# Token tiles from a block-ordered copy, constants asked for later, and six PSUM banks for the early projection

## The chip, the cores and the metric

The kernel runs on one core of one Trainium2 chip. The metric is the device time of one execution in microseconds (us), and lower is better. The engines are named as the profile names them: PE is TensorE (PEld its weight loads), DVE is VectorE, ACT is ScalarE, POOL is GpSimd and SP is SyncE, which here issues the DMA transfers.

## The reference

A transformer block on 48 x 48 tokens of 768 channels (float32 throughout) is followed by a block of Fourier mixing. Cut to what matters:

```
xn  = layernorm(x)                                  # 2304 tokens x 768
q, k, v = split(xn @ qkv_w + qkv_b)                 # 12 heads of 64
attn = softmax(q k^T / 8 + rel_h(q) + rel_w(q))     # 2304 x 2304 for each head
x   = x + (attn v) @ proj_w + proj_b
x   = x + gelu(layernorm(x) @ mlp_w1 + mlp_b1) @ mlp_w2 + mlp_b2
f   = rfft2(x)                                      # over the 48 x 48 grid
f   = softshrink(relu(f w1 + b1) w2 + b2)           # complex, 8 blocks of 96 channels
out = irfft2(f) + x
```

## The kernel before, in words

Tokens are worked on in groups of 384, six in all, and each group as three tiles of 128 rows. The order of tokens in the first stages is by blocks: group `g` holds eight rows `h` of the grid, and its tile `b` holds the sixteen columns `w` of one third of each of these rows. The view `blocks` (L180) of `x` describes this, so that one tile of 128 tokens is gathered from eight runs of sixteen tokens.

**The first stage** is `queries_keys_values`. Its order on PE and on SP is the order in which the program is written; the order on DVE, ACT and POOL is set by the framework's scheduler. `arrive(g)` asks SP for the three tiles of a group (L388, 384 KB each). `normal(t)` normalises one tile on DVE, with one small ScalarE step between: two statistics (L116), their aggregate (L118), the square root on ACT (L120), a reciprocal (L121) and the scaling (L124). `channels_first(g)` transposes the group on PE (L403, with the constant `ident`) and copies the result out of PSUM to `main` (L406 on DVE, L410 on ACT, both with the constant `vec`). `sums_of_tokens` (L172 on DVE) makes the sums of a seven-product matrix scheme from two groups, and `left` (L154 to L157 on POOL) those of the weights. `queries_and_keys` then runs the seven products (L446 on PE, four PSUM banks, emptied by L424 to L428, L455 and L457), and `values` does the same for the values (L477, L485, L487). The results go out to DRAM (L458, L489).

The queue of SP begins in this order: `ident` (L81), `vec` (L83), six token tiles (L388), and two pairs of weight loads (L364) of 384 KB each. A pair waits until a given tile has been normalised: the list `normalised` holds the L124 of each tile in order, and the two pairs wait for entries 3 and 4 (counted from 0). Later groups of tokens are asked for from within the products of the first pass, `arrive(2)` and `arrive(3)` behind a pair of weight loads, and `arrive(4)` and `arrive(5)` in the second pass.

**Attention** follows, the longest stage. It fills all PSUM banks, and the work on PE is again in written order.

**The early projection** multiplies the attention's output by `proj_w`. `outputs(t)` loads one tile of it from DRAM (L685, tile `og`, six buffers), `residual(t)` loads the tokens (L678) and adds the bias on POOL (L679), and `projected` runs two halves of six matmuls each (L692) into a PSUM tile `pp`, to which DVE adds the residual (L696). The PSUM pool of these tiles has two buffers. Nine of the eighteen tiles are done before a branch (L732), whose condition is worked out on DVE (L712 to L717), transposed on PE (L721) ahead of tile 2, and read back. The second half of the tiles and the multilayer perceptron come behind the branch, then the Fourier stages.

Of the kernel before, what the change touches and what calls it, by code (L numbers as in the profile page):

```python
# [15 lines left out]
PSUM = bass.MemoryType.PSUM  # L16
DRAM = bass.MemoryType.DRAM

P = 128
HW = 48  # L20
T = HW * HW
NT = T // P
C = 768
# [21 lines left out]
def block_then_afno(  # L45
    ctx: ExitStack,
    tc: tile.TileContext,
    x,
    qkv_w,
    proj_w,  # L50
    mlp_w1,
# [19 lines left out]
    nc = tc.nc  # L71
# [6 lines left out]

    const = ctx.enter_context(tc.tile_pool(name="const", bufs=1))
    ident = const.tile([P, P], F32, name="ident")  # L80
    nc.sync.dma_start(out=ident, in_=c_ident)  # L81
    vec = const.tile([P, V_N], F32, name="vec")
    nc.sync.dma_start(out=vec, in_=vecs)  # L83
    eps = const.tile([P, 1], F32, name="eps")
    nc.vector.memset(eps, 1e-5)
    ones = const.tile([P, P], F32, name="ones")
# [66 lines left out]
    def left(eng, a11, a12, a21, a22, s):  # L153
        eng.tensor_tensor(s[0], a21, a22, ALU.add)  # L154
        eng.tensor_tensor(s[1], s[0], a11, ALU.subtract)  # L155
        eng.tensor_tensor(s[2], a12, s[1], ALU.subtract)
        eng.tensor_tensor(a21, a11, a21, ALU.subtract)  # L157
# [19 lines left out]
        return [a[:, :, at] for a in (*blocks, *(xs[:, i] for i in range(3)))]  # L177


    blocks = x.rearrange("(a h b w) c -> a b h w c", h=8, b=3, w=16)  # L180

    def by_rows(a):

# [5 lines left out]
    with ExitStack() as flag_scope:  # L189
# [11 lines left out]
        with ExitStack() as att:  # L201
# [120 lines left out]
            def queries_keys_values(qkv):  # L322
# [38 lines left out]
                def weights_of(pr, slot, behind=None):  # L361
                    w, ws = pairs[slot]
                    for i in range(2):
                        load = nc.sync.dma_start(  # L364
                            out=w[:, :, i],
                            in_=qkv_w[:, ds(i * C + pr * P, P)].rearrange("(c p) f -> p c f", p=P),
                        )
                        if behind is not None:
                            tc.add_manual_dep(
                                load.ins, behind.ins.name,  # L370
                                mybir.DependencyInfo(
                                    mybir.DependencyClass.Sync, mybir.DependencyReason.DATA
                                ),
                                reason="tokens first",
                            )
                    left(
                        nc.gpsimd, w[:, 0:3, 0], w[:, 3:6, 0], w[:, 0:3, 1], w[:, 3:6, 1],
                        [ws[:, i] for i in range(3)],
                    )
                    return w, ws  # L380
# [3 lines left out]
                def arrive(g):  # L384

                    x3 = b_pool.tile([P, 3, C], F32, name="x3", tag="terms")
                    for i in range(3):
                        nc.sync.dma_start(out=x3[:, i], in_=blocks[g, i])  # L388
                    arrived[g] = x3

                normalised = []
# [96 lines left out]
                        t = 6 * p + 3 * (j - 1) + i  # L488
                        nc.sync.dma_start(out=v_d[ts(t, P), ts(k - 1, CH)], in_=o)  # L489

                for g in range(2):
                    arrive(g)
                for t in range(6):
                    normal(t)
                orders = []
# [6 lines left out]
                    orders.append(work)  # L502

                pairs_left = [i for work in orders for kind, i in work if kind == 0]
                ahead = [weights_of(pairs_left.pop(0), i, normalised[3 + i]) for i in range(2)]
                slot = 0
                for p in range(T // TB):
                    for g in (2 * p, 2 * p + 1):
# [29 lines left out]
            with tc.manual_schedule(engines={mybir.EngineType.PE, mybir.EngineType.SP}):  # L538
# [80 lines left out]
                with tc.manual_schedule(engines={mybir.EngineType.Activation}):  # L619
                    for n, (pr, c, u) in enumerate(runs):  # L620
# [19 lines left out]
                        if pr < NC - 1:  # L640
                            if (c, u) in ((3, 1), (4, 0), (4, 1)):
                                i = 2 * (2 * (c - 3) + u - 1)
# [33 lines left out]
        def residual(t):  # L676

            nc.sync.dma_start(out=x1[:, t, :], in_=x[ts(t, P), :])  # L678
            nc.gpsimd.tensor_tensor(x1[:, t, :], x1[:, t, :], pb, ALU.add)  # L679

        def outputs(t, og=None):

            if og is None:
                og = pj.tile([P, NC, P], F32, name="og")
            nc.sync.dma_start(out=og, in_=oT[:, ts(t, P)].rearrange("(c p) t -> p c t", p=P))  # L685
            return og

        def projected(psum, t, og):
            for k in range(2):
                pp = psum.tile([P, CH], F32, name="pp", tag="o")  # L690
                for c in range(NC):
                    nc.tensor.matmul(  # L692
                        pp, og[:, c, :], pw[:, c, ts(k, CH)], start=(c == 0), stop=(c == NC - 1)
                    )
                half = x1[:, t, ts(k, CH)]
                nc.vector.tensor_tensor(half, pp, half, ALU.add)  # L696
# [2 lines left out]

        EARLY = NT // 2  # L700
        with tc.tile_pool(name="ps_flag", bufs=1, space=PSUM) as psum, tc.tile_pool(
            name="ps_early", bufs=2, space=PSUM
        ) as psum_early, tc.manual_schedule(engines={mybir.EngineType.PE}):
            early = {t: outputs(t) for t in range(3)}
            pb = pj.tile([P, C], F32, name="pb", bufs=1)
            nc.sync.dma_start(out=pb, in_=proj_b[0, :].partition_broadcast(P))
            b2 = pj.tile([P, C], F32, name="b2_early", bufs=1)
            nc.sync.dma_start(out=b2, in_=mlp_b2[0, :].partition_broadcast(P))
            residual(0)
            projected(psum_early, 0, early[0])  # L710
            total = flag_pool.tile([P, 2], F32, name="total")
            nc.vector.tensor_reduce(total[:, 0:1], sums, AX.X, ALU.add)  # L712
            nc.vector.tensor_reduce(total[:, 1:2], inverse, AX.X, ALU.add)
            within = flag_pool.tile([P, 2], F32, name="within")
            nc.vector.tensor_scalar(within, total, BIG, None, ALU.is_lt)
            both = flag_pool.tile([P, 1], F32, name="both")
            nc.vector.tensor_tensor(both, within[:, 0:1], within[:, 1:2], ALU.mult)  # L717
            for t in range(1, EARLY):
                if t == 2:
                    line = psum.tile([1, P], F32, name="line")  # L720
                    nc.tensor.transpose(line, both, ident)  # L721
                    all_f = flag_pool.tile([1, 1], F32, name="all_f")
                    nc.vector.tensor_reduce(all_f, line, AX.X, ALU.min)
                    all_i = flag_pool.tile([1, 1], I32, name="all_i")
                    nc.vector.tensor_copy(all_i, all_f)
                residual(t)
                projected(psum_early, t, early[t] if t in early else outputs(t))
            for t in range(EARLY, NT):
                residual(t)
            later = {t: outputs(t) for t in range(EARLY, EARLY + 3)}  # L730
        safe = nc.values_load(all_i[0:1, 0:1], min_val=0, max_val=1)
        with tc.If(safe < 1):  # L732
            with ExitStack() as att:
                xnT = main.rearrange("p (c t) -> p c t", c=NC)
                with tc.tile_pool(name="g_ln1", bufs=3) as ln1, tc.tile_pool(
                    name="g_ps_ln1", bufs=2, space=PSUM
# [24 lines left out]
                for pr in range(NC):  # L761
                    w3 = []
                    for n, name in enumerate(("g_wq", "g_wk", "g_wv")):
                        w = w_pool.tile([P, NC, P], F32, name=name)
                        nc.sync.dma_start(
                            out=w,
                            in_=qkv_w[:, ds(n * C + pr * P, P)].rearrange("(c p) f -> p c f", p=P),
# [33 lines left out]
                    for sg in range(T // SG):  # L801
# [20 lines left out]
                        for i in range(2):  # L822
                            hp = psum.tile([P, G], F32, name="g_hp", tag="m")
                            for r in range(8):
                                h = sg * 16 + i * 8 + r
# [13 lines left out]
                        for i in range(2):  # L839
                            wp = psum.tile([P, 24, 16], F32, name="g_wp", tag="m")  # L840
                            for r in range(24):
                                w = i * 24 + r
# [15 lines left out]
                        for j in range(2):  # L858
                            for qt in range(SG // P):
# [27 lines left out]
                                for kg in range(NT // 3):  # L887
# [20 lines left out]
                                    out=oT[ds(pr * P + 64 * j, 64), ds(sg * SG + qt * P, P)],  # L908
                                    in_=ot[rows, :],
# [226 lines left out]
    with ExitStack() as sp:  # L1136
# [35 lines left out]
        for t in range(2):  # L1172
            nc.sync.dma_start(
                out=d2[ts(t, HW)].rearrange("p n o -> p (n o)"),
                in_=fb2[t, :].partition_broadcast(HW),
# [242 lines left out]
def _laid_out(x, given):  # L1418

    import numpy as np  # L1420

    w = {name: np.asarray(a) for name, a in given.items()}

    def columns(v):
        return v.reshape(-1, P).T

    vecs = np.concatenate(
        [
            columns(v)
            for v in (  # L1430
                w["L0_conv_ln1_g"],
                w["L0_conv_ln1_b"],
                w["L0_conv_ln2_g"],
                w["L0_conv_ln2_b"],
                w["L0_conv_qkv_b"],
                w["L0_conv_mlp_b1"],
            )
        ],
        axis=1,
    )  # L1440

    rel = np.zeros((HD, 2, 112), np.float32)
    for i, name in enumerate(("L0_conv_rel_pos_h", "L0_conv_rel_pos_w")):
        rel[:, i, : 2 * HW - 1] = w[name][::-1].T
    arrays = {
        "x": np.asarray(x).reshape(T, C),
        "qkv_w": w["L0_conv_qkv_w"],
        "proj_w": w["L0_conv_proj_w"],
        "mlp_w1": w["L0_conv_mlp_w1"],
        "mlp_w2": w["L0_conv_mlp_w2"],  # L1450
        "vecs": vecs,
        "v_b": w["L0_conv_qkv_b"][None, 2 * C :],
        "proj_b": w["L0_conv_proj_b"][None],
        "mlp_b2": w["L0_conv_mlp_b2"][None],
        "rel": rel,
        "fw1": w["L1_conv_w1"].transpose(2, 0, 1, 3),
        "fb1": w["L1_conv_b1"].transpose(2, 0, 1),
        "fw2": w["L1_conv_w2"].transpose(2, 1, 0, 3),
        "fb2": w["L1_conv_b2"].reshape(2, -1),
    }  # L1460
    return {name: np.ascontiguousarray(a) for name, a in arrays.items()}
# [22 lines left out]
```

## Time and profile before

| | us |
|---|---|
| three runs | 2912.9, 2913.75, 2915.84 (median 2913.75) |
| the profiled execution, device time | 2914.89 |
| its span in the profile | 2912.8 |
| PE busy in this span | 2846.0 |
| PE busy in its first 300 us | 271.5 |
| from 1475 to 1550 us (the early projection) | 70.6 of 75 |
| mean granted PE clock | 0.997 |

The span is the time from the first to the last instruction of the profiled execution, and the device time has some 2 us around it. In a list of instructions, the times are counted from the start of the span; what stands in brackets behind an instruction is how long its engine had been idle and which work ended that. A line number is that of the kernel before. A list of waits has, for each pair of instructions, the total wait, how often it occurred and the longest.

### The profile page before, as it was taken

The page shows a single profiled execution, that of the slowest core. Times are in us where ns is not written, and L with a number is a line of the kernel's source. Part 1 is how long each engine was busy: PE and PEld are TensorE (multiplying, and loading weights), DVE is VectorE, ACT ScalarE, POOL GpSimd, SP SyncE. Part 2 cuts the span into 40 slices and gives each one's busy share as a digit, 9 for nine tenths or more (in the row PEclk, how much of TensorE's full clock was granted, in tenths as well). Part 3 has the DMA queues.
Part 4 walks back from the last instruction along what each step waited for, and adds up shares of the span by engine and source line. Part 5 has one row for each costly group of instructions (what it writes and reads, how often), then busy time and mean ns, then how long its engine had stood idle before and what let it go on. Part 6 is the DMA issues. An engine that isn't in the chain of part 4 may idle for free. (4 is left out here: it accounts for less than half of the span.)

```text
span 2912.8 us, 41244 instructions
## 1 busy us (share of the span) xinstructions
PE 2846.0 (98%) x15803; PEld 1702.9 (58%) x15803; DVE 1791.4 (61%) x2606; ACT 934.8 (32%) x1514; POOL 614.1 (21%) x564
## 2 busy tenths in 40 slices
PE   7999999999999999999999999999999999999998
PEld 4555655555555555555555555555555555556884
DVE  5342327777777777777733666675666666666564
ACT  1011116656656565665510211112110211012341
POOL 2302110000000000000043233243323322322441
PEclk9999999999999999999999999999999999999999
DMA  4423276173461725535252112112211211113235
GB/s 121 155 82 125 87 162 123 31 137 69 71 140 31 132 55 95 116 51 90 63 179 77 38 55 65 57 52 87 65 55 55 98 54 55 55 55 117 76 96 184
DMA packets 204451, 255.59 MB, mean 88 GB/s; under 512 B 21906, under 2 KB 182610, under 8 KB 202710
## 3 DMA queue, kind: packets, MB, share of 16 engines
q1 hardware_dynamic: 201786, 249.18, 33.6%
q10 hardware_dynamic: 2460, 3.69, 0.4%
q8 instruction: 127, 2.08, 0.3%
q14 instruction: 78, 0.64, 0.1%
HBM read 136.88 MB, written 52.20 MB: 65 GB/s over the span
## 5 line engine op out<-in xcount | busy, mean ns | idle before, releaser
L635 DVE TENSOR_TENSOR acc<-acc,main 128x768 f32<-128x768 f32 x576 | 551.8, 958 | 206.4 <-ACT main L569 149.8
L569 ACT ACTIVATE main<-sp 128x768 f32<-128x768 f32 x648 | 520.2, 811 | 139.5 <-PE sp L565 132.4
L565 PE MATMUL sp<-terms,select 64*128 64x384 f32 x1296 | 413.1, 631 | 0.0
L1051 DVE TENSOR_TENSOR main<-o,main 128x384 f32<-128x384 f32 x540 | 299.0, 556 | 39.8 <-PE o L1049 1.2
L989 PE MATMUL h<-shared,w 128*128 128x384 f32 x864 | 296.6, 486 | 0.8 <-issue 0.8
L559 PE MATMUL sp<-shared 64*128 64x384 f32 x1296 | 268.1, 490 | 2.5 <-DVE o L457 2.2
L559 PE MATMUL sp<-qT,kT 64*128 64x384 f32 x1296 | 266.3, 488 | 0.2
L612 POOL TENSOR_TENSOR inverse<-inverse,rden 128x384 f32<-128x384 f32 x36 | 46.3, 1287 | 1014.4 <-DVE rden L609 944.8
L446 PE MATMUL m<-main 128*128 128x384 f32 x756 | 246.7, 488 | 5.5 <-DVE main L172 2.7
L989 PEld LDWEIGHTS h<-shared,w 128*128 128x128 f32 x864 | 164.1, 190 | 116.4 <-issue 2.3
L989 PE MATMUL h<-shared,w1s 128*128 128x384 f32 x648 | 226.7, 486 | 0.0
L582 PE MATMUL op<-main,shared 128*64 128x384 f32 x1296 | 221.2, 488 | 0.0
L582 PE MATMUL op<-main,v 128*64 128x384 f32 x1296 | 219.9, 488 | 0.0
L995 ACT ACTIVATE hT<-c,vec 128x384 f32<-128x384 f32 x108 | 66.4, 615 | 465.9 <-DVE c L1001 465.7
L446 PEld LDWEIGHTS m<-main 128*128 128x128 f32 x756 | 142.6, 190 | 107.1 <-issue 7.7
L1001 DVE TENSOR_TENSOR c<-h,u 128x384 f32<-128x384 f32 x108 | 60.1, 557 | 212.4 <-PE h L989 212.4
L1049 PE MATMUL o<-w,hT 128*128 128x384 f32 x432 | 175.9, 489 | 4.0 <-DVE mv L118 2.0
L1049 PE MATMUL o<-w2s,hs 128*128 128x384 f32 x432 | 175.0, 487 | 1.4 <-DVE hs L155 1.1
L565 PEld LDWEIGHTS sp<-terms,select 64*128 64x128 f32 x1296 | 125.7, 187 | 84.1 <-issue 0.4
L989 PEld LDWEIGHTS h<-shared,w1s 128*128 128x128 f32 x648 | 123.1, 190 | 85.8
L154 POOL TENSOR_TENSOR w1s<-w 128x384 f32<-128x384 f32 x36 | 36.8, 1022 | 605.0 <-PE o L1049 386.9
L559 PEld LDWEIGHTS sp<-shared 64*128 64x128 f32 x1296 | 117.9, 187 | 61.2 <-issue 22.8
(158 smaller groups left out, 3857.7 us busy)
## 6 DMA issues: line engine op xcount, KB each, us to landing
w<-in_mlp_w_dram SPq DMA_DIRECT2D x72, 768.0 KB
terms<-col_parts SPq DMA_DIRECT2D x432, 72.0 KB
terms<-row_hi SPq DMA_DIRECT2D x216, 72.0 KB
terms<-row_lo SPq DMA_DIRECT2D x216, 72.0 KB
main<-in_qkv_w_dram SPq DMA_DIRECT2D x36, 384.0 KB
z<-zt SPq DMA_DIRECT2D x48, 192.0 KB
x<-in_x_dram SPq DMA_DIRECT2D x18, 384.0 KB
k_d<-o SPq DMA_DIRECT2D x36, 192.0 KB
```

Of the source, the lines that this page charges most:

```text
L446: nc.tensor.matmul(bank, a[:, c, :], b[:, c, :], start=(first and c == 0), stop=(c == 2), skip_group_check=not first,)
L559: nc.tensor.matmul(sp[:, j, :G], kT[at, ts(kt, P)], qT[at, ts(c, G)], start=True, stop=False,)
L565: nc.tensor.matmul(sp[:, j, :G], select[at, a % 2], ready[pr, c][at, a // 2, b], start=False, stop=True,)
L569: nc.scalar.activation(p, sp[:, :, :G], AF.Exp, scale=HD**-0.5)
L582: nc.tensor.matmul(op[ts(j, 64)], v[:, kt0 + i, ts(j, 64)], ps[i][:, j, :], start=(kt0 + i == 0), stop=(kt0 + i == NT - 1),)
L612: nc.gpsimd.tensor_tensor(inverse, inverse, rden, ALU.add)
L635: nc.vector.tensor_tensor(acc, made[0] if kt == 1 else acc, p, ALU.add)
L989: nc.tensor.matmul(bank[i], a[:, c, :], b[:, c, :], start=(start and c == 0), stop=(c == 2), skip_group_check=not start,)
L995: nc.scalar.activation(h[:, i, ts(k, G)], src, AF.Gelu, bias=col(V_B1 + 2 * n + i))
L1001: nc.vector.tensor_tensor(t, src, other, ALU.add)
L1049: nc.tensor.matmul(bank[k], a, b, start=start, stop=True, skip_group_check=not start)
L1051: nc.vector.tensor_tensor(dst, bank[k], dst, ALU.add)
```

## The change

Four things are edited. The program gets a second DRAM input, `x_blocks`, which holds the tokens already in block order, and `arrive` loads from it, so that a tile of 128 tokens is one run of 128 rows. The loads of `ident` and `vec` are issued after the first three token tiles and no longer at the very start. The first two pairs of weights wait for the entries 2 and 4 of `normalised`, where they waited for 3 and 4. And the PSUM pool of the early projection has six buffers for `pp` where it had two. The residual (L678) still reads `x`.

```diff
     ident = const.tile([P, P], F32, name="ident")
-    nc.sync.dma_start(out=ident, in_=c_ident)
     vec = const.tile([P, V_N], F32, name="vec")
-    nc.sync.dma_start(out=vec, in_=vecs)
...
-    blocks = x.rearrange("(a h b w) c -> a b h w c", h=8, b=3, w=16)
...
                     for i in range(3):
-                        nc.sync.dma_start(out=x3[:, i], in_=blocks[g, i])
+                        nc.sync.dma_start(out=x3[:, i], in_=x_blocks[ts(3 * g + i, P), :])
...
-                for g in range(2):
-                    arrive(g)
+                arrive(0)
+                nc.sync.dma_start(out=ident, in_=c_ident)
+                nc.sync.dma_start(out=vec, in_=vecs)
+                arrive(1)
                 for t in range(6):
                     normal(t)
...
-                ahead = [weights_of(pairs_left.pop(0), i, normalised[3 + i]) for i in range(2)]
+                ahead = [weights_of(pairs_left.pop(0), i, normalised[2 + 2 * i]) for i in range(2)]
...
         with tc.tile_pool(name="ps_flag", bufs=1, space=PSUM) as psum, tc.tile_pool(
-            name="ps_early", bufs=2, space=PSUM
+            name="ps_early", bufs=6, space=PSUM
         ) as psum_early, tc.manual_schedule(engines={mybir.EngineType.PE}):
...
         "x": np.asarray(x).reshape(T, C),
+
+        "x_blocks": np.asarray(x).reshape(6, 8, 3, 16, C).transpose(0, 2, 1, 3, 4).reshape(T, C),
```

More of the change, by code (lines that the diff above doesn't have):

```diff
@@ L48, in block_then_afno @@
     x,
+    x_blocks,
     qkv_w,
```

## The prediction

> **What bounds the kernel now.** I read the page first: TensorE (PE) is busy almost all of the span, and the chain that ended last is PE lines. So a time goes down only where PE stands still on that chain.
>
> ```profile
> span 2912.8 us, 41244 instructions
> ...
> PE 2846.0 (98%) x15803; PEld 1702.9 (58%) x15803; DVE 1791.4 (61%) x2606; ACT 934.8 (32%) x1514; POOL 614.1 (21%) x564
> ...
> PE   7999999999999999999999999999999999999998
> ```
>
> The span less PE's busy time is 67 us, most of it in the first slice (the 7) and the last. So the second view is the list of waits for 0 to 45 us: total wait, number of times, longest.
>
> ```profile
> PE m L403 <- DVE x L124: 15.4, 2, 14.4
> ...
> DVE stats L116 <- DMA x<-in_x_dram: 9.8, 6, 4.4
> ...
> PE m L403 <- DVE main L406: 4.4, 2, 4.1
> ```
>
> PE waits for a normalised tile (L124), and VectorE (DVE) waits for the tokens six times. The third view, the timeline of the same stretch, gives the instants (start, length, engine, instruction, idle before).
>
> ```profile
> 0.73 0.39 SPq L81 DMA_DIRECT2D ident<-in_c_ident_dram  x1
> 1.18 0.42 SPq L83 DMA_DIRECT2D vec<-in_vecs_dram  x1
> 1.65 4.13 SPq L388 DMA_DIRECT2D x<-in_x_dram  x6
> ...
> 7.23 1.02 DVE L116 BATCH_NORM_STATS2 stats<-x 128x6 f32<-128x384 f32 x2 [4.41 <-DMA x<-in_x_dram]
> ...
> 12.56 1.02 DVE L116 BATCH_NORM_STATS2 stats<-x 128x6 f32<-128x384 f32 x2 [1.41 <-DMA x<-in_x_dram]
> ...
> 20.44 0.56 DVE L116 BATCH_NORM_STATS2 stats<-x 128x6 f32<-128x384 f32 x1 [1.38 <-DMA x<-in_x_dram]
> ```
>
> Tile follows tile at about 2.66 us (7.23, 9.89, 12.56): this is the pace of arrival, since DVE idles before each. PE's first projection matmul (L446) starts only at 28.61. The fourth view, a table of short windows, tells why: from 12 to 14 us the DMA engines' mean share is 0.52 at 147 GB/s, and 384 KB (393 thousand bytes) at 147 GB/s are 2.67 us.
>
> Two later gaps on PE matter, both in the timeline. At 84.88 PE had stood for want of a PSUM bank that DVE frees; DVE was stuck in its order behind statistics of tokens that came late:
>
> ```profile
> 81.75 1.02 DVE L116 BATCH_NORM_STATS2 stats<-x 128x6 f32<-128x384 f32 x2 [3.94 <-DMA x<-in_x_dram]
> ...
> 84.88 19.59 PE L446 MATMUL m<-main 128*128 128x384 f32 x60 [1.86 <-DVE rstd L121]
> ```
>
> And in the early projection PE fills two banks, then waits for the first L696 to empty one:
>
> ```profile
> 1475.99 8.01 PE L692 MATMUL pp<-col_parts,og 128*128 128x384 f32 x24 [0.73 <-ACT rden L602]
> ...
> 1485.43 0.55 DVE L696 TENSOR_TENSOR main<-pp,main 128x384 f32<-128x384 f32 x1
> ...
> 1486.03 8.01 PE L692 MATMUL pp<-col_parts,og 128*128 128x384 f32 x24 [2.04 <-DVE main L696]
> ```
>
> **What the Trainium skill says.** (1) "DMA: Bandwidth & Descriptors", section "Why a DMA increments its semaphore by 16 and not by 1": a copy runs on the largest number of engines up to 16 that divides the slowest dimension of both its access patterns. The old source is 8 x 16 x 768 against 128 destination rows, so 8 engines; the new one is 128 x 768, so 16. The trace agrees: a share of 0.52 is 8.3 of 16. (2) "GPSIMD Engine Reference", section "1. Specifications": GpSimd shares its SBUF interfaces with VectorE where that has two SBUF inputs or a two-port mode. The trace agrees for two inputs: L172 takes about 1.94 us (four in 7.77 us at 28.5) while L154 to L157 run on POOL, and 1.35 us when POOL has none of them (161.7); POOL's pieces take 2.1 in place of 1.0 us. (3) "Perfetto Trace Analysis", section "Optimization Strategy": a gap that repeats on the engine that should be saturated can mean too few PSUM buffers. The gap at 1486 is of that kind but stands once: later L696 keep up.
>
> **The change part by part.** Each engine's instructions stand in the same order as before, but for SP's: three token loads, ident, vec, three token loads.
>
> *Tokens on 16 engines, constants behind them.* Spacing: half of 2.67, 1.33 us; the two ends are 0.96 (410 GB/s, which the windows show at 1490 to 1492 us, where L678 loads 128-row tiles of the same size) and 2.67 (no gain). First tile: before, 5.58 us from issue (1.65) to statistics (7.23), of which 2.67 transfer, so 2.9 of latency. Now the issue is at 0.73: 0.73 + 2.9 + 1.33 = 5.0 at the late end. Ident, first in the queue, had DMA busy within 0.8 to 1.3 us of its issue, so a load with nothing ahead may do with 1.8 of latency in all: 3.8 at the early end. I take 4.6. The third tile then comes at 4.6 + 2 x 1.33 = 7.3; DVE's two earlier tiles (1.27 us each: 7.23 to the end of L118 at 8.49) end at 7.1, so arrival still decides narrowly. Gain there: 12.56 - 7.3 = 5.3 us.
>
> After this, DVE waited 0.19, 1.04 and 1.38 us for tiles four to six: 2.6 us. Without waits DVE wants them 2.5, 4.1 and 5.3 us after the third tile's statistics start (15.21, 17.87, 20.44 less 12.56 and less the waits up to then). They come after ident and vec (97 KB, 0.3 to 0.7 us) at 1.6 to 2.0, then 1.33 apart: up to 3.4 and 4.7. All in time, so the 2.6 us go too. From there to 28.61 DVE's chain has no DMA in it and is kept. Start of L446: 28.61 - 5.3 - 2.6 = 20.7, **7.9 us earlier** (7.1 to 8.7 for the two latencies and a few tenths of SP issue).
>
> Ident is wanted at the end of the first L124, 1.8 us after the third tile; it comes 0.2 to 0.4 after it. Vec is wanted by L410 and L406, later still. The move costs nothing under that cover; without it, PE would be late by what ident is late.
>
> *First weights behind tiles 2 and 4, not 3 and 4.* Two loads of 384 KB. SP issues the first pair now at about 7.3 + 3.8 (12.56 to 16.36, end of the third L124) = 11.1, and behind tile 3 it would be 13.7. Before, issue at 21.61 led to POOL at 26.74, 5.1 us; so they serve from 16.3 on. PE wants them at 20.7: 4.4 us of cover, so zero either way. They stand behind the six token loads in the same queue and so delay none. The second pair keeps its place. POOL now works on the first pair at 16 to 20 us, beside DVE's last L124 and L406. No row shows L124 beside POOL: 0 to 1.3 us lost (two L124 of 0.66 doubled); L406 reads PSUM and took 0.68 beside POOL at 27.9. I take 0. POOL's second pair still runs beside L172, so that price stays; at most 1.4 us could come back (PE's wait for L172).
>
> *Later token loads.* At 75.27 SP issues three, behind weights; the first is used at 81.75, the second at 83.66 after 0.65 us of wait. With 1.33 spacing: the first at 80.4, its statistics and L118 to 81.65, the second at 81.75, L116 to 82.3, L457 (0.6) to 82.9, and PE resumes at 83.05 in place of 84.88; it was free at 83.02. **1.8 us.** The set at 60 us held no matmul (PE runs through 55.63 to 83.02), nor does the one at 204.
>
> *Six banks.* PE goes into tile 1 at once: **2.0 us.** Its next bank reuse is tile 3, at about 1500, long after the first L696 (1485.98). L721, which DVE's L717 (ends 1488.5) must precede, is reached at 1491.7 in place of 1493.9: no wait. The four added banks were score banks, last read by ScalarE (L569) at 1463. Loads of og wait for their six buffers: tile 6's is issued at 1484.52, 38 us ahead of use. DVE's L696 is no longer what PE waits for, and the 3.86 us at the branch (L732) stay. Ends: 0 (if a new bank were late) and 2.7 (PEld's wait).
>
> Sum: 7.9 + 1.8 + 2.0 = 11.7 us. The profiled execution was 2914.89 us with a span of 2912.8 (2.1 around it), so 2903.2 with a span of 2901.1; the median of the three runs is 1.1 lower, 2913.75, so **2902.0 us**.
>
> **The rivals.** *A: the start turns bound by DVE or POOL* (the POOL collision, last three tiles late by a first latency of 5 us). Startup brings 4 to 6 us: 2904 to 2906. For it: DVE's margin is a few tenths at every tile. Against: its order keeps the waits' slack. *B: the loads do not speed up*, because HBM and not eight engines set 147 GB/s. Then only the place ahead of ident and vec (about 0.9) and the banks (2.0) remain: 2911. Against: 410 GB/s at 1490 us and 290 at 26 us. *C: slower through the clock.* PE's work gets denser, and the granted clock, 1.00 in most windows but 0.98 at 1550 to 1630 and 0.99 at 300 to 600, falls. Of 2846 busy us each 0.1% costs 2.8 us: below a mean of 0.993 (from 0.997) the gain is gone, and below 0.991 the kernel is over 5.8 us slower; at 0.990 it would give 2922. For it: the dips exist. Against: work of 12 us spread less is no reason for so much.
>
> **How the numbers follow.** The forecast 0.78, A 0.10, B 0.05, C 0.05, 0.02 elsewhere. A measurement here can tell about 0.2%, 5.8 us. The forecast and A are faster by more (0.88, and a little of the rest: 0.90); B is within; C is slower. The range: early end 7.9 + 0.8, 1.4 from L172, 0.7 from PEld, so 2899; late end A's 2906, with a run's noise of 1 us each side: 2898 to 2907.
>
> **What would show it.** Right: DMA share near 1 in the first 10 us, the third tile's statistics at 7 to 7.7, no L116 wait over 0.3 after it, L446 from 20 to 21.5, no gap at about 75 (84.88 less the shift), L692 without the wait for L696. Wrong: share still 0.5 (B), L116 waits in tiles four to six or L172 and L124 longer (A), a PEclk below 0.993 (C), or a new wait of L721 or L692 at the projection.

## The result, and the profile after

The changed kernel takes 2902.43 us (median of five runs, 2900.36 to 2903.35) against 2913.75 us (2912.88 to 2915.84): the ratio is 0.9953, with a 95% interval of 0.9942 to 0.9963. The forecast was 2902.0. In the profiles the span goes from 2912.8 to 2900.4 us, 12.4 less, and PE's busy time hardly changes (2846.0 before, 2848.4 after). In the changed kernel the line numbers of the first stage are lower by one or two: L388, L403, L446, L172 and L124 of before are L386, L401, L444, L171 and L123.

The page after:

```profile
span 2900.4 us, 41241 instructions
...
PE 2848.4 (98%) x15803; PEld 1703.9 (59%) x15803; DVE 1789.9 (62%) x2606; ACT 936.2 (32%) x1514; POOL 612.4 (21%) x564
```

The list of waits of the changed kernel for 0 to 45 us (total, number, longest):

```profile
PE m L401 <- DVE x L123: 8.8, 2, 8.2
...
DVE stats L115 <- DMA x<-in_x_blocks_dram: 1.1, 1, 1.1
```

PE's wait for normalised tiles goes from 15.4 to 8.8 us. In this stretch DVE now waits for tokens once, for the very first tile. The timeline of the changed kernel's start shows the same as instants:

```profile
0.73 1.34 SPq L386 DMA_DIRECT2D x<-in_x_blocks_dram  x3
...
2.11 0.43 SPq L490 DMA_DIRECT2D ident<-in_c_ident_dram  x1
...
3.87 1.02 DVE L115 BATCH_NORM_STATS2 stats<-x 128x6 f32<-128x384 f32 x2 [1.06 <-DMA x<-in_x_blocks_dram]
...
6.36 0.96 DVE L115 BATCH_NORM_STATS2 stats<-x 128x6 f32<-128x384 f32 x2
...
19.95 7.91 DVE L171 TENSOR_TENSOR main<-main 128x1152 f32<-128x1152 f32 x4
...
20.08 2.20 PE L444 MATMUL m<-main 128*128 128x384 f32 x6 [0.44 <-DVE main L404]
...
23.86 8.39 PE L444 MATMUL m<-main 128*128 128x384 f32 x25 [1.57 <-DVE main L171]
```

The third tile's statistics start at 6.36, with no bracket: DVE came to them from its own work and not from a wait. The projection starts at 20.08 in place of 28.61.

Two lines of the tables of short windows (stretch, length, busy time of PE, PEld, DVE, ACT and POOL with the number of instructions, granted clock, and last the DMA engines' mean share and GB/s) show the loads themselves, each while tokens come. The first is of the kernel before, the second of the changed one:

```profile
12.00:14.00 2.00, 0.00 (x0) 0.00 (x0) 1.44 (x6) 0.15 (x1) 0.00 (x0) 1.00 0.52 147
```

```profile
6.00:8.00 2.00, 0.00 (x0) 0.00 (x0) 1.97 (x8) 0.59 (x2) 0.00 (x0) 1.00 1.03 398
```

A share a little above 1 is read here as all 16 engines at work. The second late set of tokens still lets DVE wait, but for less than PE has in hand; PE runs through (timeline, 45 to 100 us):

```profile
44.66 55.63 PE L444 MATMUL m<-main 128*128 128x384 f32 x172
...
71.12 1.02 DVE L115 BATCH_NORM_STATS2 stats<-x 128x6 f32<-128x384 f32 x2 [1.84 <-DMA x<-in_x_blocks_dram]
```

In the early projection two tiles go through without a break, up to the transpose of the flag:

```profile
1464.50 15.75 PE L692 MATMUL pp<-col_parts,og 128*128 128x384 f32 x48 [0.73 <-ACT rden L602]
...
1473.90 0.55 DVE L696 TENSOR_TENSOR main<-pp,main 128x384 f32<-128x384 f32 x1
...
1480.09 0.27 PE L721 MATMUL line<-ident,both 128*1 128x128 f32 x1
```

The first L696 comes 9.4 us after PE's start here as there (1473.90 less 1464.50; 1485.43 less 1475.99). It is as late as it was; PE no longer needs it.

The lead of the changed kernel, from its trace against that of before at the same instructions:

| place | before | after | lead |
|---|---|---|---|
| first product of the first stage | 28.61 | 20.08 | 8.5 |
| second product | 32.24 | 23.86 | 8.4 |
| L428 (after: L426) before the second late token set | 77.25 | 68.73 | 8.5 |
| L428 (after: L426) after it | 92.90 | 82.27 | 10.6 |
| start of the early projection | 1475.99 | 1464.50 | 11.5 |
| L721 | 1493.88 | 1480.09 | 13.8 |
| a wait of L1280, at the beginning of the end | 2874.78 | 2860.04 | 14.7 |
| end of the span | 2912.8 | 2900.4 | 12.4 |

### The profile page after: what moved, and what is told of

It is laid out like the page before. It is cut to its first block, busy times and chain, and to the rows that moved or that the text cites. A ratio compares the mean times of both kernels' runs of the same rounds, so it can differ in the third digit from the quotient of the medians.

```text
span 2900.4 us, 41241 instructions
## 1 busy us (share of the span) xinstructions
PE 2848.4 (98%) x15803; PEld 1703.9 (59%) x15803; DVE 1789.9 (62%) x2606; ACT 936.2 (32%) x1514; POOL 612.4 (21%) x564
## 5 line engine op out<-in xcount | busy, mean ns | idle before, releaser
L444 PE MATMUL m<-main 128*128 128x384 f32 x756 | 246.0, 487 | 3.8 <-DVE main L171 2.9
L444 PEld LDWEIGHTS m<-main 128*128 128x128 f32 x756 | 142.9, 190 | 104.3 <-issue 5.0
```

Source lines behind the costliest of these rows:

```text
L444: nc.tensor.matmul(bank, a[:, c, :], b[:, c, :], start=(first and c == 0), stop=(c == 2), skip_group_check=not first,)
```

## The experiments

Theory 1 was the prediction's: 16 DMA engines in place of 8 carry most of the gain, the place of the constants little, the place of the first weights nothing, the banks about 2 us. Theory 2 had another cause: the order of requests in the first experiments, the long unbroken runs of the copy in the two with a gap. The ratios below are to the kernel before on the same chip, whose median was 2914.99 us on one chip and 2915.07 on the other.

**The copy alone** (kernel before, tokens from `x_blocks`):

```diff
-                        nc.sync.dma_start(out=x3[:, i], in_=blocks[g, i])
+                        nc.sync.dma_start(out=x3[:, i], in_=x_blocks[ts(3 * g + i, P), :])
```

> The kernel before, with the tokens from the block-ordered copy and nothing else. Theory 1 (16 DMA engines in place of 8 carry nearly the whole gain): tiles land at most 1.3 us apart, the first statistics start at about 5.1 us (in the changed kernel 3.87, and here the loads are issued 0.92 later and behind 97 KB), the first L446 of the projection at 21.2 in place of 28.61, no gap of 1.9 us on PE in the second token set: 9 to 10.4 us less than before, about 2904. Theory 2 (the order of constants and weights carries it): under 3 us less, about 2911.

Measured: 2906.4 us, ratio 0.9971 (0.9960 to 0.9983). First statistics at 5.18, first product at 21.48, no gap in the second token set; the wait of L692 is still there (2.09 us). The gain is about 8.5 us (5 to 12 by the interval). That is just under theory 1's 9 to 10.4; theory 2's under 3 us is out.

**The constants alone** (kernel before, `ident` and `vec` behind three tiles):

```diff
-                for g in range(2):
-                    arrive(g)
+                arrive(0)
+                nc.sync.dma_start(out=ident, in_=c_ident)
+                nc.sync.dma_start(out=vec, in_=vecs)
+                arrive(1)
```

> The kernel before, with ident and vec asked for behind the first three token tiles and nothing else. Theory 1: the first statistics come at about 6.0 in place of 7.23, but tiles four to six now stand behind the constants and still come 2.66 us apart, so the last one at about 19.9 in place of 20.44 and the first L446 at 28.0: 0.6 us less, within noise of 2913.5. Theory 2: several us less.

Measured: 2915.43 us, ratio 1.0005 (0.9997 to 1.0014): no change that can be told. Its trace surprised. The first product starts at 24.29, 4.3 us earlier than in the first profile of before, because the tiles here arrive about 2.07 us apart and not 2.66. Against a profile of the kernel before whose loads ran at the same 209 GB/s, told of below, the product starts 0.6 us earlier (24.29 and 24.88), as expected. With the fast loads the earlier place shows more: the copy alone has its first statistics at 5.18 and its first product at 21.48, the changed kernel at 3.87 to 4.11 and 19.76 to 21.10 in four profiles. This was not timed on its own.

**The banks alone** (kernel before):

```diff
-            name="ps_early", bufs=2, space=PSUM
+            name="ps_early", bufs=6, space=PSUM
```

> The kernel before with six PSUM buffers for the early projection and nothing else. Theory 1: the wait of 2.04 us of L692 for L696 is gone and no other takes its place: 2.0 to 2.3 us less, about 2911.5. Rival: the branch behind the ninth tile waits for something else that ends no earlier, so that PE's idle time before the branch grows from 3.86 by 2 us and the time stays at 2913.7.

Measured: 2911.99 us, ratio 0.9988 (0.9981 to 0.9994). The timeline of this kernel shows the unbroken run:

```profile
1478.23 15.75 PE L692 MATMUL pp<-col_parts,og 128*128 128x384 f32 x48 [0.73 <-ACT rden L602]
...
1487.40 0.55 DVE L696 TENSOR_TENSOR main<-pp,main 128x384 f32<-128x384 f32 x1
```

PE's idle time at the branch is 3.98 us against 3.86: the rival, a wait that grows there by 2 us, is out. In the six profiles with two buffers the wait of L692 was 1.9 to 3.7 us, in the eight with six buffers it was absent.

**The weights alone** (kernel before):

```diff
-normalised[3 + i]
+normalised[2 + 2 * i]
```

> The kernel before with the first pair of weights waiting for tile 2 in place of tile 3 and nothing else. Theory 1: the pair lands about 5 us earlier and is not what PE waits for: L446 still starts at 28.6, no change (2913.7 within 0.7). Rival a: POOL's first four pieces leave the stretch of L172, L172 shortens and PE's wait of 1.43 us before the second product goes: up to 1.4 us less. Rival b: the 768 KB get in the way of the last token tiles: L446 up to 2.6 us later.

Measured: 2915.3 us, ratio 1.0006 (0.9997 to 1.0014). PE's wait before the second product is 1.27 us and the four L172 take 7.61, so rival a does not show. Nor does rival b: from the third tile's statistics to the first product it is 14.3 us (11.38 to 25.65), and 14.4 in a profile of the kernel before at the same pace. The first product stands at 25.65, by the faster pace of the tokens again.

**A gap in the copy, in two grains.** To part the number of engines from the unbroken run, the copy got one unused row behind each run of 16 rows, or behind each run of 8:

```diff
# gap_8: stored as (18, 8, 17, C)
-in_=x_blocks[ts(3 * g + i, P), :]
+in_=x_blocks[3 * g + i, :, :16]
# gap_16: stored as (18, 16, 9, C)
-in_=x_blocks[ts(3 * g + i, P), :]
+in_=x_blocks[3 * g + i, :, :8]
```

> The changed kernel with a gap in the copy: each tile lies as 8 runs of 16 rows with one unused row behind each run, so the source's slowest dimension is 8 as before the change, while the rows still stand in block order next to each other. Theory 1 (the number of engines decides): DMA share near 0.5 while tokens come, tiles 2.1 to 2.7 us apart, first L444 between 24 and 27, that is 4 to 7 us later than in the changed kernel, and the gap in the second token set is back: 2908 to 2911 on the chip of the first runs. Theory 2 (long, neighbouring runs of memory decide): as the changed kernel, L444 at 20.1.

> The changed kernel with a gap in the copy, in the other grain: each tile lies as 16 runs of 8 rows with one unused row behind each run, so more and shorter runs than before the change, but a slowest dimension of 16. Theory 1: DMA share near 1, tiles at most 1.3 us apart, L444 at 20.1, the time of the changed kernel. Theory 2: no better than with 8 runs, L444 at 24 or later.

Measured: 2911.68 us, ratio 0.9994 (0.9986 to 1.0003), with eight runs; 2906.52 us, ratio 0.9972 (0.9960 to 0.9984), with sixteen. With eight runs the gain of the tokens is gone: the first product starts at 25.72, as theory 1 said, and the 1.7 us that the ratio leaves are about what the banks bring, which this kernel keeps. The short windows, first with eight runs:

```profile
12.00:14.00 2.00, 1.25 (x4) 0.66 (x5) 2.00 (x5) 0.00 (x0) 0.00 (x0) 1.00 0.52 209
```

with sixteen runs:

```profile
6.00:8.00 2.00, 0.00 (x0) 0.00 (x0) 1.27 (x4) 0.59 (x2) 0.00 (x0) 1.00 1.11 267
```

The slowest dimension sets the share: 0.52 with 8, about 1 with 16, as the Trainium skill's "DMA: Bandwidth & Descriptors" has it in "Why a DMA increments its semaphore by 16 and not by 1". The pages agree in another way. First the line of the kernel with eight runs, then that with sixteen:

```profile
DMA packets 204451, 255.59 MB, mean 88 GB/s; under 512 B 21906, under 2 KB 182610, under 8 KB 202710
```

```profile
DMA packets 204595, 255.59 MB, mean 88 GB/s; under 512 B 22050, under 2 KB 182754, under 8 KB 202854
```

The kernel before has the first line too, and the changed kernel the second. The 144 packets more are all under 512 B, and 144 is 18 token loads times 8. This fits one small packet for each of eight more engines in each load.

But theory 1 is only half of it. With sixteen broken runs the engines are about as busy as in the changed kernel and carry 243 to 267 GB/s where those carry 323 to 398 (windows of 2 us from 2 to 8; from 8 to 10 us it is 293 with the gap, when the changed kernel has nearly all its tokens). Tiles come 1.6 to 1.7 us apart, the first product starts at 22.84, between the forecasts of the two theories (25.72 with eight runs, 20.08 without a gap), and 0.71 us of the gap in the second token set is back (2.19 us with eight runs). Of the 2.8 us up to the first product, some 0.8 is not the rate of the loads: DVE and POOL met in this profile, as told below. SP also takes 0.66 us to issue one such load, and 0.45 us for an unbroken one (1.98 and 1.34 us for three). More or smaller packets are not the reason for the lower rate, since the page of the changed kernel has the same counts in each class of size. Whether the runs or the memory beneath cost it was not parted, and the rate rests on one profile.

**The changed kernel again, and repeats of both.** Eight-engine loads had come at different paces, and the first profile of the changed kernel had lost 2.3 us of its lead in the last 40 us. Three more profiles of the changed kernel and two more of the kernel before were taken (no edit).

> The changed kernel once more, for its last 40 us. In its first profile the stretch from the first L1280 wait at 2860.04 to the end is 40.4 us, in the kernel before and in the four with one part of the change 37.5 to 38.8. Theory 1 (arrival of zo from DRAM varies between executions, nothing of the change reaches it): 37.5 to 40.5 here, most likely near 38, and a span near 2898. Rival (the earlier start moves the last loads into each other's way): 40 or more again.

> The kernel before, a second profile, for two things that differ between executions: the pace of its 8-engine token loads (2.66 us a tile in the first profile, but about 2.07 in two of the four kernels that still have them) and the length of the last stretch, from the wait of L1280 to the end (38.0 us). Theory 1 (both vary between executions of one kernel): pace anywhere from 2.0 to 2.7, last stretch 37.5 to 39, first L446 between 25.5 and 29. Rival (the pace belongs to the kernel): 2.66 and 28.6 again.

> As the second profile of the kernel before. Theory 1: pace 2.0 to 2.7, last stretch 37.5 to 39. Rival: pace 2.66 again.

> The changed kernel, a third profile, for the same two things. So far its last stretch took 40.4 and 39.4 us, the kernels with a part of the change 37.5 to 38.9. Theory 1 (chance): 37.5 to 40.5, the mean of four profiles not more than 1 us above the others. Rival (the whole change lengthens the last stretch): 39.4 or more. First L444 at 20 to 21.1 either way, since DVE and no longer the loads sets it.

> As the third profile of the changed kernel: last stretch 37.5 to 40.5 by chance, 39.4 or more by the rival; first L444 at 20 to 21.1.

Measured: 2902.1 us, ratio 0.9957 (0.9944 to 0.9970), for the timed one. The single profiles took 2913.31 and 2919.89 us (before), 2904.63 and 2899.48 (changed). The pace belongs to the execution and not to the kernel. The windows of the kernel before, second profile:

```profile
12.00:14.00 2.00, 0.95 (x2) 0.36 (x2) 2.00 (x6) 0.11 (x1) 0.00 (x0) 1.00 0.52 209
```

and third profile:

```profile
12.00:14.00 2.00, 0.00 (x0) 0.00 (x0) 1.61 (x6) 0.30 (x1) 0.00 (x0) 1.00 0.52 151
```

The same share of 0.52, with 209 or 151 GB/s in it; the first product follows at 24.88 and 28.91. In the changed kernel it stands at 20.08, 21.10, 20.39 and 19.76. So the lead at the start is 3.8 to 9.2 us, as the execution before falls. In one of these, at 21.10, DVE and POOL met:

```profile
15.82 1.00 POOL L154 TENSOR_TENSOR main<-main 128x384 f32<-128x384 f32 x1
15.82 1.42 DVE L123 TENSOR_SCALAR x<-x,mv,rstd 128x768 f32<-128x768 f32 x1
```

The last scaling takes 1.42 in place of 0.67 us while POOL keeps its 1.00; in the first profile of the changed kernel it was POOL that took 1.41. The Trainium skill's "GPSIMD Engine Reference" ("1. Specifications") names a conflict of the two in a two-port mode, with which the slowing agrees; the mode itself is not in the trace. With sixteen broken runs the last scaling took 1.44 us in the same way.

The last stretch (from L1280's wait to the end) took 38.0, 38.1 and 37.8 us before, 40.4, 39.4, 39.4 and 38.5 in the changed kernel, and 37.5 to 38.9 in the kernels with other edits. The first two ranges do not overlap and their means differ by 1.5 us, but the changed kernel's shortest (38.5) lies within the last range. The rival's 39.4 or more is missed by that one, and chance's limit of 1 us above the others is missed by the mean, which is 1.3 us above them. A third candidate is the granted clock, which these expectations left out. In the windows of the last 40 us it was 0.82 in the first profile of the changed kernel, where PE was busy for 31.8 us, and 0.94 with 28.5 us in that of before. PE also waited less for the DMA of `zo` there (3.2 against 5.9 us from 2840 us on), so a later arrival is not what lengthened that stretch in this profile; the lower clock goes with it. But the kernel before had 0.90 with 38.1 us and the changed kernel 0.92 with 39.4, so the clock alone does not order them. This stays open.

**The second pair later** (changed kernel; the second L171 is returned by `sums_of_tokens`):

```diff
-                ahead = [weights_of(pairs_left.pop(0), i, normalised[2 + 2 * i]) for i in range(2)]
+                ahead = [weights_of(pairs_left.pop(0), 0, normalised[2])]
...
-                    sums_of_tokens(xt, xs)
+                    summed = sums_of_tokens(xt, xs)
+                    if p == 0:
+                        ahead.append(weights_of(pairs_left.pop(0), 1, summed[1]))
```

> The changed kernel, in which the second pair of first weights waits for the second L171 (the sum t2 that PE's second product needs) in place of tile 4, so that POOL's pieces for it no longer run beside the L171. Theory 1 (the two engines slow each other): the four L171 take about 5.4 us in place of 7.9, PE's wait of 1.57 us before its second product falls to about 0.3, the pair is ready at about 31.5 and PE's second weight pair is first needed at about 31: 1.2 us less than the changed kernel. Rival (the pair comes too late): PE waits up to 2 us at about 32 for POOL, and nothing is gained or up to 1 us lost.

Measured: 2899.83 us, ratio 0.9953 (0.9940 to 0.9966). Its timeline:

```profile
20.32 5.35 DVE L172 TENSOR_TENSOR main<-main 128x1152 f32<-128x1152 f32 x4
...
23.28 23.14 PE L446 MATMUL m<-main 128*128 128x384 f32 x71 [0.61 <-DVE main L172]
```

In this kernel L172 and L446 are the L171 and L444 of the changed one. The four sums take 5.35 us in place of 7.91 (7.25 to 8.11 in the four profiles of the changed kernel) and PE's wait 0.61 in place of 1.57 us (1.22 to 1.77). From there PE runs on, so the pair is not late. The mechanism is shown. Its gain of about 1 us is not: the interval overlaps most of that of the changed kernel.

## Why the prediction was right, step by step

**Start.** Forecast: 7.9 us earlier; measured 8.5 in the first pair of profiles. *First tile at 4.6*: it came at 3.87, near the early end of 3.8, so the 2.9 us of latency taken over from before was too long, and the term was 0.7 too large. Waiting behind the constants is a small part of that: from issue to first statistics it is 3.14 us here and 3.54 with the copy alone, whose constants come first. SP's quicker issue (0.45 against 0.69 us for a load) is another; the rest was not parted. *The third tile at 7.3, set by arrival*: it was 6.36, before the 7 to 7.7 that the prediction gave as its sign, and set by DVE's own 1.25 us a tile. Arrival did not decide in this profile; in the third one DVE waited 0.39 us for the tile (6.80). *Waits of 2.6 us for tiles four to six go*: they went. *The rest of DVE's chain is kept, 13.4 us from the third tile to the first product*: it took 13.7. *Late constants and earlier weights cost nothing*: right, no wait for `ident` or `vec` appears, and both edits alone are within their intervals of no change.

What failed in the reasoning is the term "half of 2.67", though it cost the sum little. It takes the doubled engines as all that changes, and the kernel with sixteen runs shows that the unbroken source counts too: its tiles came 1.6 to 1.7 us apart. Without a gap, 393 thousand bytes at the 367 to 398 GB/s of 4 to 8 us are 1.0 to 1.1 us a tile (an estimate), which is below DVE's 1.25, and so DVE took over. And 2.67 was itself one of two paces. Of three profiles of before, two have it; with the other the start would have given 4.8 us (24.88 to 20.08). The start's 8.5 us is measured against the same slow profile that the forecast was built on. The forecast's range held the smaller gain by its rival A, for another reason.

**Later tokens.** Forecast 1.8; the lead grows by 2.1 across the second set. Not foreseen were 0.6 us at the first values product, where PE's wait for POOL's L155 fell from 0.95 to 0.36 us, and about 0.3 us between 203 and 285 us. The first of these looks like chance: the same wait was 0.33 and 0.75 us in the other profiles of before and 0.23 to 0.79 in those of the changed kernel.

**Banks.** Forecast 2.0; the lead grows by 2.3. L721 found its input ready and no new wait came, as argued.

**Sum.** 11.7 was forecast; the trace has 13.8 at L721, 14.7 before the end and 12.4 at the end. So the close agreement of 2902.0 and 2902.4 is partly luck: the terms were 2.1 us too small up to L721, another 0.9 us up to the last stretch has no account, and the last stretch, which the prediction left alone, was 2.3 us longer.

**Rivals.** A's POOL collision exists, at 0.75 us on one scaling, within the 0 to 1.3 allowed. B is out as it was put: the share is near 1 and the rate up to 398 GB/s; that memory plays no part is not shown. C is out for the whole span: the mean clock was 0.996 to 0.998 in all profiles. The dips of the clock stood at other places after: one of 0.98 from 1475 to 1550 us, and a deep one, the 0.82 of the last 40 us.

## What to carry to other kernels

Read the DMA share of a stretch before its bandwidth: a steady share of 0.52 here meant that the shape of the load kept half the engines out, and the slowest dimension of the source (8 or 16) decided it. Give a load an unbroken source as well, since sixteen engines on broken runs carried some 30% less in the one profile taken. And where a stage is bound by arrival, look at the work behind it first: here DVE's 1.25 us a tile took over in most profiles, so still faster loads would bring little at the start (argued from the waits, not tested).

## What the runs showed of the hardware that was not expected

Eight-engine loads of one kernel on one chip ran at 147 to 151 GB/s in one execution and at 204 to 209 GB/s in another (windows of 2 us from 6 to 14), at the same DMA share of 0.51 to 0.52. Other kernels with such loads, on other chips, ran at 147 to 151 or at 197 to 209 GB/s, and one (the weights alone) went from about 160 to 209 GB/s at 8 to 10 us. The cause was not found. It moves the first product by 4 us, a third of what the whole change brings, so one profile is not enough to measure a start.
